# One step of Strassen's method in all six matrix products of a four-layer convolution kernel

## The chip, the cores and the metric

The kernel runs on one core of a Trainium2 chip. Its time is the device time of one execution in microseconds; the time before is the median of three runs. Profiles are of one execution each, and windows in them are counted from the start of the profiled span, which is some 2 us shorter than the device time.

## What is computed

The input is one image of 1024 channels by 64 x 64 pixels in f32. Four layers follow one another, each of the form `x = x + layer(group_norm(x))`:

```python
# layer 0: layer norm over the 64 x 64 of a channel, then a scan over the 1024 channels
dt  = softplus(einsum('bsdc,c->bsd', xn, dt_w) + dt_b)      # one decay per channel and image row
out = scan over s:  h = exp(-exp(log_A) * dt) * h + xn       # written as a masked product of cumsums
# layer 1 and layer 3: 1x1 convolution
out = einsum('oi,nihw->nohw', weight, x) + bias
# layer 2: input projection to 3 x 1024 channels, then a selective scan, then an output projection
x_ssm, res, gate = split(silu(in_proj_w @ x + b), 3)
xf  = silu(conv1d_3_taps(x_ssm))                             # along the 4096 pixels
dt, B, C = dbc_w @ xf + dbc_b                                # 2 heads x (1 + 8 + 8) rows
y   = selective_scan(xf, dt, B, C) in a data-dependent order of the pixels, per head
out = silu(out_proj_w @ (y * silu(gate) + res) + out_proj_b)
```

Six products of a 1024 x 1024 matrix with a 1024 x 4096 image carry nearly all of the arithmetic: layer 1, the three thirds of the input projection (x, res, gate), the output projection, layer 3.

## The kernel before

The image lies in SBUF throughout, as eight blocks `X[nb]` of 128 partitions x 8 channel tiles x 512 pixels (2 MB each). The program is written against a tile framework: its scheduler orders each engine's instructions by a cost estimate and by the order of the text, and it adds the waits; every engine then runs its own queue in order. Nearly all plain transfers are issued from the SP queue, indirect ones from GpSimd.

- **Layer 0** (lines 268 to 312): per block, ScalarE normalizes, TensorE transposes (`l0pt`) and sums the decay rows (`l0pd`), ScalarE and one small GpSimd add (`l0m`, L296) make the softplus, the result goes to HBM (`a_d`) and comes back broadcast (`l0a`, L302), VectorE scans (L304), TensorE transposes back (`l0pb`), VectorE adds into `X` and takes the statistics for the next norm (`take_stats`, L114).
- **Layers 1 and 3** (`pointwise`, L367): the whole weight matrix is loaded, then for each block and each of the eight output tiles `o` a group of eight matmuls over `k` fills one PSUM bank (`pm`), and one VectorE instruction (L387) adds bias and image back into `X`.
- **Ranking** (`rank_work`, L317): layer 2 needs the pixels in the order of a score. VectorE counts, for every pixel, the smaller scores (`hit`, L331; ties in `eq`, L342), in pieces of 1024 scores (`srow`). The steps are cut into a generator; `rank_steps` queues `each` of them behind a given instruction. In layer 1 there are 3 behind each of the 64 evictions, the rest lie in the x third of layer 2.
- **Layer 2, x third** (L435): eight tiles of output channels, each over the eight blocks, weights of one output tile at a time (`wt`). Per 128 x 512 result: silu, a conv of three taps on VectorE (L450, L453), silu, four transposes (`l2pt`, L462) and four matmuls with the block of pixels as the stationary side and the 34 columns of dt/B/C as the moving one (`l2pd`, L463), summed by VectorE over the eight tiles (L476). The transposed tokens go to HBM (`tok_d`).
- **Layer 2, res/gate and scan** (L517): 74 steps of the scan (`weigh`, `apply`) gather 128 tokens, build a 128 x 128 matrix on TensorE (`pr`, `pg`), VectorE, ScalarE and GpSimd (`cd`, L557), multiply (`py`) and scatter to `y_d`. Between them stand the res and gate products (`res_gate`), written to `res_d` and `sg_d`.
- **Layer 2, output** (L613): per block, `y`, `sg` and `rs` are loaded in eight tiles each, `y` is transposed (`ypt`), and eight groups of matmuls (`op`, L639) follow.

Every product of a 128 x 128 weight tile with 512 columns is one matmul call; f32 matmuls show as two records in the trace.

Of the kernel before, what the change touches and what calls it, by code (L numbers as in the profile page):

```python
# [23 lines left out]
NB = 8  # L24
# [14 lines left out]


_PAR = [("b1", CT), ("bin", OI), ("dww", 3 * CT), ("dwb", CT), ("bout", CT), ("b3", CT),
        ("logA", NB), ("lnw", NT), ("lnb", NT), ("dtw", 1), ("dtb", 1),
        ("Alog", S), ("D", 1), ("mob", 4 * HEADS), ("dbcb", HEADS * NF)]
# [19 lines left out]
def tile_net(ctx: ExitStack, tc: tile.TileContext, x, par_d, cst_d, w1_d, win_d, dbcw_d, wout_d, w3_d, out):  # L63
    nc = tc.nc
    const = ctx.enter_context(tc.tile_pool(name="const", bufs=1))
    xpool = ctx.enter_context(tc.tile_pool(name="xres", bufs=1))
    psum = ctx.enter_context(tc.tile_pool(name="psum", bufs=1, space=PSUM))
    phase = [None]
# [6 lines left out]
    def ps_mm(name):  # L75
        return ps_tile("mm", 3, name)

    def ps_tp(name):
        return ps_tile("tp", 2, name)

    def ps_g(name):
        return ps_tile("g", 2, name)

    def ps_y(name):
        return ps_tile("y", 1, name)

    x1_d = dram.tile([C, N], F32, name="x1_d")
# [19 lines left out]
    X = [xpool.tile([P, CT, FB], F32, name=f"X{nb}") for nb in range(NB)]  # L107
    for nb in range(NB):
        nc.sync.dma_start(X[nb], x[:, nb * FB : (nb + 1) * FB].rearrange("(ct p) n -> p ct n", p=P))  # L109
# [147 lines left out]
    for nb in range(NB):  # L257
        for ct in range(CT):
            take_stats(nb, ct)

# [6 lines left out]

    with tc.issue_after(exp_ln.ins), tc.tile_pool(name="l0", bufs=2) as l0, \
            tc.tile_pool(name="ps0", bufs=2, space=PSUM) as ps0:
        for nb in range(NB):  # L270
            xt = l0.tile([P, TPB, C], F32, tag="xt", name=f"l0xt{nb}")
# [39 lines left out]
            for ct in range(CT):  # L311
                take_stats(nb, ct)

# [53 lines left out]
    def pointwise(name, w_d, bias_name, each=0, store=None):  # L367
        scale, bias = group_norm(f"gn{name}")
        with tc.tile_pool(name=f"{name}w", bufs=1) as wp, tc.tile_pool(name=f"{name}x", bufs=12) as xp, \
                tc.tile_pool(name=f"{name}p", bufs=1, space=PSUM) as pp:  # L370
            phase[0] = pp
            w = wp.tile([P, CT, C], F32, name=f"{name}_w")
            for k in range(CT):
                nc.sync.dma_start(w[:, k, :], w_d[k])
            for nb in range(NB):
                xn = []
                for k in range(CT):
                    t = xp.tile([P, FB], F32, tag="xn", name=f"{name}xn{nb}_{k}")
                    nc.scalar.activation(t, X[nb][:, k, :], AF.Identity,  # L379
                                         bias=bias[:, k : k + 1], scale=scale[:, k : k + 1])  # L380
                    xn.append(t)
                for o in range(CT):
                    pm = ps_mm(f"{name}pm{nb}_{o}")
                    for k in range(CT):
                        nc.tensor.matmul(pm, w[:, k, o * P : (o + 1) * P], xn[k],  # L385
                                         start=(k == 0), stop=(k == CT - 1))
                    last = nc.vector.scalar_tensor_tensor(  # L387
                        X[nb][:, o, :], pm, pcol(bias_name, o), X[nb][:, o, :], ALU.add, ALU.add)
                    if store is None:
                        last = take_stats(nb, o)  # L390
                    rank_steps(each, last)
                dst = x1_d if store is None else store
                nc.sync.dma_start(dst[:, nb * FB : (nb + 1) * FB].rearrange("(ct p) n -> p ct n", p=P), X[nb])

    rank_pool = tc.tile_pool(name="rank", bufs=2, side="right")
    work = rank_work(rank_pool.__enter__())
# [6 lines left out]
    pointwise("l1", w1_d, "b1", each=3)  # L403


    ps2 = tc.tile_pool(name="ps2", bufs=1, space=PSUM)
    phase[0] = ps2.__enter__()
    scale2, bias2 = group_norm("gn2")
    for nb in range(NB):
        for ct in range(CT):  # L410
            sc, bi = scale2[:, ct : ct + 1], bias2[:, ct : ct + 1]
            if ct % 2 == 0:
                nc.scalar.activation(X[nb][:, ct, :], X[nb][:, ct, :], AF.Identity, bias=bi, scale=sc)
            else:
                nc.vector.tensor_scalar(X[nb][:, ct, :], X[nb][:, ct, :], sc, bi, ALU.mult, ALU.add)

    with tc.tile_pool(name="l2w", bufs=2) as l2w:

        def in_proj_weights(oc):
            wt = l2w.tile([P, CT, P], F32, tag="wt", name=f"wt{oc}")  # L420
            nc.sync.dma_start(wt, win_d[oc])
            return wt

        def in_proj(wt, oc, nb):
            pm = ps_mm(f"ip{oc}_{nb}")
            for k in range(CT):
                nc.tensor.matmul(pm, wt[:, k, :], X[nb][:, k, :], start=(k == 0), stop=(k == CT - 1))  # L427
            return pm


        with tc.tile_pool(name="l2a", bufs=2) as pa, tc.tile_pool(name="l2acc", bufs=1) as pacc:
            dbcw = pacc.tile([P, CT, HEADS * NF], F32, name="dbcw")
            nc.sync.dma_start(dbcw, dbcw_d)
            acc = pacc.tile([P, NT, HEADS * NF], F32, name="acc")
            for oc in range(CT):  # L435
                wt = in_proj_weights(oc)
                xs = pa.tile([P, N + 2], F32, tag="xs", name=f"xs{oc}", bufs=2)
                nc.vector.memset(xs[:, 0:1], 0.0)
                nc.vector.memset(xs[:, N + 1 : N + 2], 0.0)
                h, c0 = oc // 4, (oc % 4) * P  # L440
                for nb in range(NB + 1):
                    if nb < NB:
                        pm = in_proj(wt, oc, nb)
                        nc.scalar.activation(xs[:, 1 + nb * FB : 1 + (nb + 1) * FB], pm, AF.Silu,  # L444
                                             bias=pcol("bin", oc))
                    if nb == 0:
                        continue
                    j = nb - 1
                    cv = pa.tile([P, FB], F32, tag="cv", name=f"cv{oc}_{j}")
                    nc.vector.tensor_scalar(cv, xs[:, j * FB : (j + 1) * FB], pcol("dww", 3 * oc),  # L450
                                            pcol("dwb", oc), ALU.mult, ALU.add)
                    for t in (1, 2):
                        nc.vector.scalar_tensor_tensor(  # L453
                            cv, xs[:, j * FB + t : (j + 1) * FB + t], pcol("dww", 3 * oc + t), cv,
                            ALU.mult, ALU.add)
                    xf = pa.tile([P, FB], F32, tag="xf", name=f"xf{oc}_{j}")
                    nc.scalar.activation(xf, cv, AF.Silu)
                    pt = ps_tp(f"l2pt{oc}_{j}")
                    pd = ps_g(f"l2pd{oc}_{j}")
                    for q in range(TPB):  # L460
                        blk = xf[:, q * P : (q + 1) * P]
                        nc.tensor.transpose(pt[:, q * P : (q + 1) * P], blk, ident)  # L462
                        nc.tensor.matmul(pd[:, q * HEADS * NF : (q + 1) * HEADS * NF], blk, dbcw[:, oc, :],  # L463
                                         start=True, stop=True)
                    xt = pa.tile([P, TPB, P], F32, tag="xt", name=f"l2xt{oc}_{j}")
                    nc.scalar.copy(xt.rearrange("p q c -> p (q c)"), pt)
                    nc.sync.dma_start(
                        tok_d[h * N + j * FB : h * N + (j + 1) * FB, c0 : c0 + P].rearrange(
                            "(q p) c -> p q c", p=P), xt)
                    got = pd[:, : TPB * HEADS * NF].rearrange("p (q f) -> p q f", q=TPB)  # L470
                    at = acc[:, j * TPB : (j + 1) * TPB, :]
                    if oc == 0:
                        more = par[:, PAR["dbcb"]].unsqueeze(1).to_broadcast([P, TPB, HEADS * NF])
                    else:
                        more = at
                    last = nc.vector.tensor_tensor(at, got, more, ALU.add)  # L476

                    rank_steps(3, last)
            rank_steps(2 * NT * HEADS * CT, last)
            rank_pool.__exit__(None, None, None)  # L480


            with tc.tile_pool(name="l2f", bufs=1) as pf:
                for h in range(HEADS):
                    f = acc[:, :, h * NF : (h + 1) * NF]
# [31 lines left out]
        with tc.tile_pool(name="l2b", bufs=2) as pb, tc.tile_pool(name="l2h", bufs=1) as ph:  # L517
            G2 = [ph.tile([P, P], F32, name=f"G{i}") for i in range(2)]
            for g in G2:
                nc.gpsimd.memset(g, 0.0)  # L520
# [218 lines left out]
```

## Time and profile before

The median is 3389.95 us (3389.55 to 3391.72). The stages, from the trace:

| stage | from, us | to, us | TensorE busy, us | VectorE busy, us |
|---|---|---|---|---|
| load, statistics | 0 | 60 | 1.6 | 51.4 |
| layer 0 | 60 | 301 | 150.9 | 153.0 |
| layer 1 | 301 | 752 | 443.3 | 308.8 |
| layer 2, x third | 752 | 1300 | 533.6 | 300.0 |
| layer 2, res/gate and scan | 1300 | 2398 | 1091.7 | 303.4 |
| layer 2, output | 2398 | 2932 | 479.3 | 176.8 |
| layer 3 | 2932 | 3388 | 443.1 | 50.1 |

How to read the profile: a group of instructions names its line, engine and operation, what it writes and reads (`out<-in`), the shape, the number of records, the busy time, the mean time of one, and the idle time of its engine just before it with what ended that idle time. Matmuls overlap, so the time of one matmul is longer than the distance between two. The chain of waits is followed back from the last instruction; its rows are start, length, and what it was.

### The profile page before, as it was taken

The numbers are of one execution on the slowest core, as the hardware profiler recorded it, in microseconds if no ns is written. First come the engines' busy times: TensorE is split into PE (matmuls) and PEld (weight loads), VectorE is DVE, ScalarE is ACT, GpSimd is POOL, SyncE is SP. The second block draws the span as 40 slices with busy tenths as digits, with TensorE's granted clock in tenths as the row PEclk, the third lists the DMA queues.
The fourth block names the chain that finished last, engine by engine and source line by source line (L and its number), as shares of the span: only waits on it lengthen the run. The fifth ranks groups of instructions, "written<-read, shape, count | busy, mean of one in ns | idle before, by whom it ended". The sixth has DMA issues, their size and how long they took to land.

```text
span 3387.6 us, 23688 instructions
## 1 busy us (share of the span) xinstructions
PE 3143.4 (93%) x8417; PEld 1413.5 (42%) x8417; DVE 1343.5 (40%) x2744; ACT 924.4 (27%) x1242; POOL 328.3 (10%) x305
## 2 busy tenths in 40 slices
PE   2675999989999999999999999999699999999998
PEld 0333444444555554444444444444344444444443
DVE  6667777377775222222222222322133333211111
ACT  2661101004222223444444544554100000110100
POOL 0100000200002101222222222221000000000000
PEclk9886999999999999999999999999899999999999
DMA  5323011121111114222222222224723323101011
GB/s 206 89 71 98 32 55 53 34 64 38 44 44 47 38 41 77 82 73 77 76 78 79 77 73 73 86 73 152 271 75 110 114 75 116 65 25 50 36 39 50
DMA packets 190271, 258.91 MB, mean 76 GB/s; under 512 B 37817, under 2 KB 103673, under 8 KB 190154
## 3 DMA queue, kind: packets, MB, share of 16 engines
q1 hardware_dynamic: 176266, 216.70, 19.8%
q0 software_dynamic: 13888, 40.70, 3.7%
q8 instruction: 67, 1.10, 0.1%
q14 instruction: 50, 0.41, 0.0%
HBM read 152.10 MB, written 105.26 MB: 76 GB/s over the span
## 4 chain that ended last, share of the span: by engine, by line
PE 86%; DVE 5%; DMA 4%; ACT 2%; issue 1%; SPq 1%; POOL 0%; DVEq 0%; ACTq 0%; POOLq 0%
PE ip L427 38%; PE l3pm L385 13%; PE l1pm L385 13%; PE op L639 11%; PE pg L571 2%; PE py L584 2%; DMA sg<-sg_d 2%; DVE l0xt L304 1%; PE l0pd L286 1%; PE l2pd L463 1%; PE l0pb L308 1%; PE pr L550 1%; PE l2pt L462 1%; PE pr L551 1%; SPq L109 1%
## 5 line engine op out<-in xcount | busy, mean ns | idle before, releaser
L427 PE MATMUL ip<-X,wt 128*128 128x512 f32 x3072 | 1373.3, 599 | 9.5 <-ACT rg L531 5.2
L427 PEld LDWEIGHTS ip<-X,wt 128*128 128x128 f32 x3072 | 574.9, 191 | 738.0 <-issue 725.0
L639 PE MATMUL op<-ym,wo 128*128 128x512 f32 x1024 | 453.6, 596 | 13.9 <-DVE ym L634 13.7
L385 PE MATMUL l3pm<-l3xn,l_w 128*128 128x512 f32 x1024 | 442.5, 595 | 3.1 <-ACT l3xn L379 3.1
L385 PE MATMUL l1pm<-l1xn,l_w 128*128 128x512 f32 x1024 | 442.1, 595 | 3.2 <-ACT l1xn L379 3.2
L331 DVE TENSOR_SCALAR_CACHE_REDUCE hit<-srow,score 128x1024 bf16<-128x1024 f32 (+7 forms) x312 | 337.4, 1081 | 15.3 <-DMA srow<-score_d 10.2
L385 PEld LDWEIGHTS l3pm<-l3xn,l_w 128*128 128x128 f32 x1024 | 195.5, 191 | 249.3 <-issue 240.8
L385 PEld LDWEIGHTS l1pm<-l1xn,l_w 128*128 128x128 f32 x1024 | 195.4, 191 | 249.1 <-issue 241.4
L639 PEld LDWEIGHTS op<-ym,wo 128*128 128x128 f32 x1024 | 189.3, 191 | 238.0 <-issue 220.7
L387 DVE SCALAR_TENSOR_TENSOR X<-l3pm,par,X 128x512 f32<-128x512 f32 x64 | 48.0, 750 | 396.3 <-PE l3pm L385 359.6
L554 DVE COPY cts<-pr 16x64 f32<-16x64 f32 x74 | 16.0, 216 | 469.8 <-PE pr L551 469.8
L531 ACT ACTIVATE rg<-ip,par 128x512 f32<-128x512 f32 x128 | 87.8, 687 | 388.8 <-PE ip L427 270.2
L642 ACT ACTIVATE os<-op,par 128x512 f32<-128x512 f32 x64 | 44.0, 687 | 486.9 <-PE op L639 439.1
L114 DVE BATCH_NORM_STATS2 stats<-X 128x6 f32<-128x512 f32 x256 | 166.8, 686 | 6.4 <-DMA X<-in_x_dram 2.2
L453 DVE SCALAR_TENSOR_TENSOR cv<-xs,par,cv 128x512 f32<-128x512 f32 x128 | 95.9, 751 | 164.2 <-ACT xs L444 161.7
L379 ACT ACTIVATE l3xn<-X,gnl_bias,gnl_scale 128x512 f32<-128x512 f32 x64 | 50.8, 810 | 336.8 <-PE l3pm L385 332.7
L379 ACT ACTIVATE l1xn<-X,gnl_bias,gnl_scale 128x512 f32<-128x512 f32 x64 | 50.9, 812 | 336.5 <-PE l1pm L385 332.6
L531 ACT ACT_TABLE_LOAD x74 | 94.9, 1283 | 156.9 <-issue 156.2
L557 POOL TENSOR_TENSOR cd<-cts,cst 16x512 f32<-16x512 f32 x74 | 76.4, 1033 | 619.3 <-DVE cts L554 619.2
L643 DVE TENSOR_TENSOR X<-X,os 128x512 f32<-128x512 f32 x64 | 44.1, 689 | 220.6 <-ACT os L642 220.6
L547 DVE TENSOR_SCALAR ds<-cst,g 128x64 f32<-128x64 f32 x74 | 21.9, 295 | 268.0 <-DMA g<-tok_d,src 251.0
L444 ACT ACTIVATE xs<-ip,par 128x512 f32<-128x512 f32 x64 | 43.9, 690 | 241.8 <-PE ip L427 241.8
(192 smaller groups left out, 2408.6 us busy)
## 6 DMA issues: line engine op xcount, KB each, us to landing
X<-in_x_dram SPq DMA_DIRECT2D x8, 2048.0 KB
l0a<-a_d SPq DMA_DIRECT2D x64, 256.0 KB
x_d<-X SPq DMA_DIRECT2D x8, 2048.0 KB
tok_d<-l2xt SPq DMA_DIRECT2D x64, 256.0 KB
res_d<-rg SPq DMA_DIRECT2D x64, 256.0 KB
sg_d<-rg SPq DMA_DIRECT2D x64, 256.0 KB
X<-x_d SPq DMA_DIRECT2D x8, 2048.0 KB
yt<-y_d SPq DMA_DIRECT2D x64, 256.0 KB
```

The costliest lines, as they stand in the source:

```text
L114: return nc.vector.bn_stats(stats[:, ct, nb, :], X[nb][:, ct, :])
L331: nc.vector.tensor_scalar(hit[:, : hi - lo], srow[:, lo:hi], sn, None, op, ALU.add, accum_out=count[:, h, b, slot : slot + 1],)
L379: nc.scalar.activation(t, X[nb][:, k, :], AF.Identity, bias=bias[:, k : k + 1], scale=scale[:, k : k + 1])
L385: nc.tensor.matmul(pm, w[:, k, o * P : (o + 1) * P], xn[k], start=(k == 0), stop=(k == CT - 1))
L387: last = nc.vector.scalar_tensor_tensor(X[nb][:, o, :], pm, pcol(bias_name, o), X[nb][:, o, :], ALU.add, ALU.add)
L427: nc.tensor.matmul(pm, wt[:, k, :], X[nb][:, k, :], start=(k == 0), stop=(k == CT - 1))
L453: nc.vector.scalar_tensor_tensor(cv, xs[:, j * FB + t : (j + 1) * FB + t], pcol("dww", 3 * oc + t), cv, ALU.mult, ALU.add)
L531: nc.scalar.activation(r, pm, AF.Silu, bias=pcol("bin", oc))
L557: nc.gpsimd.tensor_tensor(cd, cts.unsqueeze(1).to_broadcast([HEADS * S, S, LC]), eye8.unsqueeze(2).to_broadcast([HEADS * S, S, LC]), ALU.mult)
L571: nc.tensor.matmul(pg, bts, cd.rearrange("p s t -> p (s t)"), start=True, stop=True)
L584: nc.tensor.matmul(py, G, g[:, :DH], start=True, stop=True)
L639: nc.tensor.matmul(pm, wo[:, k, o * P : (o + 1) * P], ym[k], start=(k == 0), stop=(k == CT - 1))
```

## The change

All six products are done by one step of Strassen's method in Winograd's form over pairs of blocks. The weight matrix is cut into 2 x 2 quarters A11 to A22, the 1024 x 1024 pair of image blocks into B11 to B22 (rows: halves of the channels, columns: the two blocks). Seven products of halves stand for eight. It is for a smaller number of matmuls. The sums of weight quarters are made on the chip, once per matrix, by GpSimd (`sum_weights`), and go to HBM (`s_d`); the sums of image quarters (`t1` to `t4`) are made per pair (`b_sets`), by GpSimd, for a stage's first pair mostly by VectorE. The sums of products are made partly in PSUM, where a later product is accumulated on an earlier one, and partly at eviction: every output tile is written once (`put`) and added to once (`add`).

With it come: weights streamed in pieces of 512 KB, one per product, in six buffers (`weights`); only four of the eight image blocks in SBUF, the others kept in HBM (`x0_d`, `x1_d`, `x2_d`) and loaded again, with the pairs taken in alternating order so that those at hand come first (`EARLY`, `LATE`); four PSUM banks for the products, two sets of two; `each=4` rank steps behind an add in layer 1, the rest behind the convs of the x third; dt/B/C with the 34 columns as the stationary side and the pixels as the moving one, accumulated in PSUM over the eight tiles and transposed afterwards.

```diff
-    xpool = ctx.enter_context(tc.tile_pool(name="xres", bufs=1))
+    xpool = ctx.enter_context(tc.tile_pool(name="xres", bufs=4))
+    wpool = ctx.enter_context(tc.tile_pool(name="wts", bufs=6))
...
+    def sum_weights(m, pool):
+        for g in range(NG):
+            def t(name, src=None):
+                w = pool.tile([P, KH * OG * P], F32, tag=f"s_{name}", name=f"s{m}_{g}_{name}", bufs=1)
+                if src is not None:
+                    nc.gpsimd.dma_start(w, src)
+                return w
+
+            a = [t(f"a{i}", w_d[m, g, i]) for i in range(4)]
+            s3 = t("s3")
+            nc.gpsimd.tensor_tensor(s3, a[0], a[2], ALU.subtract)
+            nc.gpsimd.tensor_tensor(a[2], a[2], a[3], ALU.add)
+            nc.gpsimd.tensor_tensor(a[0], a[2], a[0], ALU.subtract)
+            nc.gpsimd.tensor_tensor(a[1], a[1], a[0], ALU.subtract)
+            for d, w in zip(s_d[m][g], (a[2], a[0], s3, a[1])):
+                nc.gpsimd.dma_start(d, w)
...
+    sum_weights(W1, sum_pool[1])
     with tc.issue_after(exp_ln.ins), tc.tile_pool(name="l0", bufs=2) as l0, \
             tc.tile_pool(name="ps0", bufs=2, space=PSUM) as ps0:
         for nb in range(NB):
+            if nb >= NB // 2:
+                load(nb, x)
...
+            if nb < NB // 2:
+                save(nb, x0_d)
...
+        def comb(name, out, one, two):
+            eng = nc.vector if first and name != "t3" else nc.gpsimd
+            B[name] = B[out] if out else [b_tile(name, k, B["name"]) for k in range(KH)]
+            for k in range(KH):
+                eng.tensor_tensor(B[name][k], B[one][k], B[two][k], ALU.subtract)
...
+            def product(to, i, name, fresh):
+                w = weights(m, g, i)
+                for o in range(OG):
+                    for k in range(KH):
+                        nc.tensor.matmul(to[o], w[:, k, o * P : (o + 1) * P], B[name][k],
+                                         start=(fresh and k == 0), stop=(k == KH - 1),
+                                         skip_group_check=True)
...
+            b = banks(two, 2)
+            product(b, 1, "b21", True)
+            out(put, 0, 0, b)
+            yield
+            a = banks(one, 1)
+            product(a, 0, "b11", True)
+            out(add, 0, 0, a)
+            yield
+            b = banks(two, 3)
+            product(b, 6, "b22", True)
+            out(put, 0, 1, b)
+            yield
+            product(a, 4, "t2", False)
+            out(put, 1, 0, a)
+            yield
+            b = banks(two, 7)
+            product(b, 5, "t3", True)
+            out(put, 1, 1, b)
+            yield
+            product(a, 3, "t1", False)
+            out(add, 0, 1, a)
+            out(add, 1, 1, a)
+            yield
+            product(b, 2, "t4", False)
+            out(add, 1, 0, b)
...
+    pointwise("l1", W1, "b1", LATE + EARLY, x0_d, x1_d, each=4)
...
+            nc.tensor.matmul(dbc[nb][: HEADS * NF, :], dbcw[:, o, :], xf,
+                             start=(count == 0), stop=(count == CT - 1))
...
+        units = run(LATE + EARLY, [WR, WG], normed(norm2), put2b, add2b, before2)
...
+        for _ in run(EARLY + LATE, [WO], make_y, put2c, add2c, before2, after2c):
```

In layers 1 and 3 both `put` and `add` are VectorE instructions. In layer 2 `put` is a ScalarE copy out of PSUM, `add` a VectorE addition; silu follows the addition.

## The prediction

> **What bounds the kernel now.** I read the page's busy line first, then its chain by engine, then the groups (shapes kept apart), then the windows, one per stage, and last the timelines of layer 0.
>
> ```profile
> PE 3143.4 (93%) x8417; PEld 1413.5 (42%) x8417; DVE 1343.5 (40%) x2744; ACT 924.4 (27%) x1242; POOL 328.3 (10%) x305
> PE 86%; DVE 5%; DMA 4%; ACT 2%; issue 1%; SPq 1%; POOL 0%; DVEq 0%; ACTq 0%; POOLq 0%
> ```
> TensorE is busy for 93% and 86% of the chain. A busy matmul row proves little by itself, so the next view matters more: the pitch.
>
> ```profile
> L427 PE MATMUL ip<-X,wt 128*128 128x512 f32 x3072 | 1373.3, 599 | 9.5 <-ACT rg L531 5.2 <-ACT X L413 3.0 <-ACT xs L444 1.3
> L385 PE MATMUL l1pm<-l1xn,l_w 128*128 128x512 f32 x1024 | 442.1, 595 | 3.2 <-ACT l1xn L379 3.2
> L331 DVE TENSOR_SCALAR_CACHE_REDUCE hit<-srow,score 128x1024 bf16<-128x1024 f32 x200 | 254.3, 1272 | 14.2 <-DMA srow<-score_d 10.2
> L463 PE MATMUL l2pd<-dbcw,xf 128*128 128x34 f32 x512 | 75.4, 239 | 0.0
> L296 POOL TENSOR_TENSOR l0m<-l0m,l0e 8x1024 f32<-8x1024 f32 x8 | 18.8, 2344 | 240.5 <-ACT l0e L295 240.5
> ```
> ```profile
> 853.80 6.95 PE ip L427 x16
> 861.87 6.95 PE ip L427 x16
> ```
> An f32 matmul leaves two records; 16 records (8 matmuls) take 6.95 us, 0.434 us each, with almost no idle before them. The mean of 599 ns is latency, not pitch. In the chain (last two lines: start, length) 1.12 us lie between two such blocks, the transposes and dt/B/C matmuls of one conv block.
>
> ```profile
> 0.00:60.00 60.00, 1.61 (x5) 1.13 (x5) 51.44 (x161) 3.39 (x8) 1.10 (x7) 1.00 0.80 291
> 301.00:752.00 451.00, 443.27 (x1028) 196.41 (x1028) 308.76 (x625) 51.11 (x65) 31.12 (x32) 0.99 0.13 45
> 752.00:1300.00 548.00, 533.63 (x1822) 275.58 (x1823) 300.03 (x628) 150.46 (x235) 33.41 (x33) 0.98 0.17 48
> 1300.00:2398.00 1098.00, 1091.67 (x2616) 451.56 (x2614) 303.43 (x823) 488.60 (x635) 243.87 (x225) 1.00 0.28 89
> 2398.00:2932.00 534.00, 479.31 (x1282) 218.25 (x1282) 176.82 (x267) 45.59 (x66) 0.00 (x0) 0.97 0.33 109
> 2932.00:3388.00 456.00, 443.07 (x1026) 196.04 (x1026) 50.06 (x76) 51.05 (x65) 0.00 (x0) 0.98 0.12 44
> ```
> Columns: PE, PEld, DVE, ACT, POOL busy, clock, DMA share, GB/s. Rows: load, layer 1, the x third of layer 2, its res/gate thirds with the scan, its output product, layer 3. Layer 0 (60 to 301) is the one stretch without a full engine. Note layer 1: VectorE already works 309 of 451 us, mostly rank counting (hit).
>
> ```profile
> 85.35 2.33 POOL L296 TENSOR_TENSOR l0m<-l0m,l0e 8x1024 f32<-8x1024 f32 x1 [80.58 <-ACT l0e L295]
> 244.75 2.35 POOL L296 TENSOR_TENSOR l0m<-l0m,l0e 8x1024 f32<-8x1024 f32 x1 [33.95 <-ACT l0e L295]
> ```
> Each image block of layer 0 passes through one small GpSimd add. GpSimd comes to it early and waits; it is never late.
>
> **What the Trainium skill says.** GPSIMD Engine Reference, section 3.1: a two-input tensor_tensor costs about 2.6 cycles an element, 4497 ns for 2048. The trace agrees: 2344 ns for 1024 a partition. DMA: Bandwidth & Descriptors, Anatomy of one DMA: a GpSimd-issued DMA costs about 2.0 us fixed plus its bytes at 436 GB/s, so 3.2 us for 512 KB (estimate); the trace has no direct DMA from GpSimd, but its indirect ones land in 2.7 and 3.8 us (median). Same page, Queues, rings and completion order: an engine takes a queue's descriptors in ring order, so a small load issued behind a 2 MB one on the SP queue waits for it; no run shows it yet.
>
> **Part by part.** *Matmuls.* 7 products for 8: 6144 records become 5376; 768 x 0.434 = 333 us off TensorE: 55.5 in each of layer 1, x, output and layer 3, 111 in res/gate.
>
> *dt/B/C as stationary side.* Per conv block four 34-column matmuls become one 512-column one (2 x 0.434 = 0.87) beside the four transposes (about 0.43 of the 1.12): 1.30 for 1.12, 64 times: +12 us. The VectorE sums it removes were hidden.
>
> *Weights streamed.* 336 loads of 512 KB, one per 6.95 us product, 75 GB/s, six buffers, so asked for some 35 us ahead. The load stage moves 291 GB/s. Hidden: 0. Half-resident image: some 60 MB more transfers; within the products hidden by prefetch; only layer 0 pays (below).
>
> *Sets of column sums.* 16 subtractions of 128x512 per pair, GpSimd, 1.17 us each (half of 2.34), within the last four products: 19 of 28 us. The first pair's 12 on VectorE at 0.69 (as L634 and L643) lie beside the first three products. 0.
>
> *Weight sums, layer 0.* The built order of GpSimd's instructions puts the 12 groups of sums among the eight l0m adds: 4 3/4 groups stand ahead of the first, about one more ahead of each next, all 12 ahead of the sixth. Behind a delayed l0m wait exp, a_d, the a loads, the scan on VectorE and layer 1. A group: four loads (issue 1 us each, as the indirect ones, landing 3.2), four adds 4 x 2.34, four stores, each buffer reused only after its store: about 22 us alone, 28 while the image loads. So the first l0m comes at 5 + 28 + 28 + 22 + 22 + 18 = 123 instead of 85, the sixth at 277 instead of 208. Then the l0 buffers' own rhythm (two blocks in 54 us), plus the SP order: the save of a block and the reload that waits for it stand ahead of the next a loads, about 14 us twice. Together I put layer 0's end at 367 instead of 301: +66. Bounds: 18 us a group with no SP effect +40; 35 us a group, sixth l0m at 408, +165.
>
> *Layer 1.* Each quadrant is now evicted twice: 64 put (0.75, as L387) + 64 add (0.69, as L310) + 64 stats (0.61 apart, eight in 4.84 in the timeline): 131 us instead of 87. And four rank steps follow each add, so of the 391 us of counting (L331 337.4 and L342 22.3, with their accumulator reads 25.9 and 5.3) the built order leaves about 310 in layer 1. With the 12 first subtractions VectorE has some 450 us of work against 387 us of products (896 x 0.434), in one queue: an eviction behind 4 counts (1.32 each) holds a PSUM bank, of which there is one spare product. VectorE becomes the bound: 450 + 20 where TensorE is behind + 15 for the srow loads that it meets unhidden = 485 instead of 451. At the end about 20 more counts lie among the group norm's steps: 25 us before x can start. +34 +20 = +54.
>
> *x third.* 389 + 64 x 1.30 = 472 of TensorE, plus some 35 of stalls: after each last product four conv blocks come at once, 4 x 2.04 us of VectorE, with few matmuls between: 507. With the norm's lead-out taken above: 548 -> 511, and the 15 us gap at 1300 closes because res products no longer wait for the scan's data: -52.
>
> *res/gate.* 1098 - 111 = 987, plus 35 (estimate): the cd path (VectorE copy, GpSimd product) has 1.8 us of slack per step and VectorE and GpSimd now carry more: -76.
>
> *Output product.* 534 - 55, and the loads of y, sg and res come 16 tiles at once: 16 x 0.77 MB at 300 GB/s, 41 us, beside four products of 28: three times 10 us, once 25; against that the eight waits of before (some 45) go: 488, -46.
>
> *Layer 3.* 456 - 55 + 1: 402, -54.
>
> Sum: 3390 + 66 + 54 - 52 - 76 - 46 - 54 = 3282. The stall terms (35 + 35 + 55 + 20 + 15 = 160) are the ones most easily under-rated, since they come from single queues looked at alone; I add a fifth of them, 33 us, for queues that meet: 3315.
>
> **Rivals.** A: TensorE stays the bound everywhere, VectorE and GpSimd keep out of its way: 3390 - 333 + 12 = 3069, to 3150 with layer 0's lower bound. For it: the idle of every engine but TensorE. Against: 450 us of VectorE in layer 1. B, slower: groups of sums cost 35 us (+165 in layer 0, 99 over mine) and the cd and conv stalls double (+70): 3484; a milder form, one of the two, 3400 to 3440. For it: GpSimd's queue is in order and unproven with direct DMAs. Against: DMA is 1 to 30% busy in layer 0. C: the weight stream falls behind on SP, behind stores that wait, half a microsecond per product: 336 x 0.5 = +168, 3483. Against: six buffers. D: gains and losses cancel to within 7 us.
>
> **How the numbers follow.** Forecast (VectorE-bound layer 1, late layer 0, 3200 to 3380) 0.62; A 0.12; D 0.04; B 0.15, C 0.07. Faster 0.74, same 0.04, slower 0.22. The range leaves out A's lower part and the worst of B and C: 3200 to 3430.
>
> **What would show it.** Right: l0m's idle turns from ACT l0e to GpSimd work, first l0m near 123; in layer 1 VectorE near 95% busy over 480 us and TensorE waiting for VectorE; matmul records 5376 at 0.43; res/gate near 1005. Wrong: layer 1 near 390 us (A), SP-fed weights as the releaser of matmuls (C), groups far from 22 us.

## The result, and the profile after

The changed kernel takes 3413.6 us (median of 4 runs, 3409.9 to 3413.8), the kernel before 3390.6 us: a ratio of 1.0065, 95% interval 1.0048 to 1.0083. It is slower by 0.65%. 3315 us and "faster" were predicted.

The page of the changed kernel, its busy line and TensorE's row of the slices:

```profile
PE 2898.8 (85%) x7315; PEld 1249.7 (37%) x7315; DVE 1672.5 (49%) x3195; ACT 1074.1 (31%) x1558; POOL 849.3 (25%) x708
PE   0454598896579699999989999998998999989999
```

TensorE is busy for 245 us less, where 321 less were expected (333 of matmuls, with 12 more for dt/B/C), and its share fell from 93% to 85%. The slices say where the idle time sits: in the first 40% of the span. To be cut alike in every kernel, the stages are taken here from fixed events: the first matmul of each group norm's statistics (image, layer 0, layer 1), ScalarE's first eviction of a res product, the first matmul of layer 3's group norm, the end. Windows at these cuts, two of the kernel before and then those of the changed kernel (us; busy PE, PEld, DVE, ACT, POOL; granted TensorE clock; DMA share; GB/s):

```profile
303.70:755.30 451.60, 443.27 (x1028) 196.41 (x1028) 309.39 (x623) 51.11 (x65) 31.12 (x32) 0.99 0.13 45
755.30:1314.40 559.10, 543.56 (x1844) 279.66 (x1844) 298.39 (x628) 152.94 (x238) 35.17 (x36) 0.99 0.17 47
```
```profile
0.00:82.70 82.70, 0.45 (x2) 0.15 (x2) 57.00 (x147) 3.17 (x6) 42.64 (x44) 1.00 1.00 381
82.70:412.70 330.00, 163.39 (x645) 83.01 (x645) 170.81 (x195) 133.91 (x172) 155.17 (x116) 0.71 0.68 224
412.70:921.60 508.90, 410.71 (x901) 175.18 (x901) 425.15 (x873) 50.65 (x65) 97.37 (x84) 0.92 0.33 113
921.60:1536.50 614.90, 525.65 (x1366) 219.30 (x1366) 293.36 (x547) 235.70 (x373) 115.69 (x90) 0.92 0.34 102
...
3014.20:3411.90 397.70, 388.54 (x900) 171.95 (x900) 104.31 (x153) 50.60 (x65) 65.50 (x52) 0.99 0.39 130
```

The lengths at the same cuts, beside the terms of the prediction:

| stage | before | after | measured | predicted |
|---|---|---|---|---|
| image, layer 0 | 55.8 + 247.9 | 82.7 + 330.0 | +109 | +66 |
| layer 1 | 451.6 | 508.9 | +57 | +54 |
| x third | 559.1 | 614.9 | +56 | -52 |
| res, gate, output | 1617.0 | 1477.7 | -139 | -122 |
| layer 3 | 456.2 | 397.7 | -58 | -54 |
| queues that meet | | | | +33 |

The second half pays what was promised, and a little more. The pitch, the distance from one matmul record to the next, is the predicted one; the chain of waits ends with this piece of layer 3:

```profile
3040.34 367.65 PE mm L476 x856
```

That is 0.430 us a record, without a gap. This pitch does not hold behind a wait. TensorE near the start of the x third, in order of time:

```profile
968.53 1.12 PE L644 MATMUL l2pt<-cst,xf 128*128 128x128 f32 x4 [10.76 <-ACT xf L641]
969.57 1.92 PE L649 MATMUL dbc<-xf,dbcw 128*34 128x512 f32 x2
971.42 1.74 PE L476 MATMUL mm<-t,w 128*128 128x512 f32 x2
972.99 0.60 PE L644 MATMUL l2pt<-cst,xf 128*128 128x128 f32 x4
973.52 1.05 PE L649 MATMUL dbc<-xf,dbcw 128*34 128x512 f32 x2
974.50 20.87 PE L476 MATMUL mm<-t,w 128*128 128x512 f32 x48
```

After a wait of 10.76 us the same four transposes and two dt/B/C matmuls take 1.12 and 1.92 us, and 4.5 us later 0.60 and 1.05. So a wait costs more here than its own length. Over a stage it shows in the windows: layer 1 and layer 3 have the same 900 records, but TensorE is busy for 411 us in one, at a granted clock of 0.92, and for 389 in the other, at 0.99.

The first half loses 222 us where 68 were expected (101 with the term for meeting queues). The waits of the whole run show the candidates (engine, line, released by: us in total, times, longest):

```profile
DVE l0xt L353 <- DMA l0a<-a_d: 117.6, 7, 53.4
ACT l2xt L652 <- DMA tok_d<-l2xt: 45.4, 6, 36.1
PE pg L820 <- POOL cd L806: 42.7, 15, 13.1
PE mm L476 <- DVE X L561: 41.7, 12, 23.3
DVE hit L382 <- DMA srow<-score_d: 41.0, 6, 25.4
```

In none of them does a matmul wait for its weights: layer 0's scan waits for its rows, a copy of the x third for its store, the scan's matmul of the res/gate stretch for GpSimd, layer 1's products for VectorE's evictions, the ranking for its score rows.

### The profile page after: what moved, and what is told of

Read it like the earlier page. It is cut to its first block, busy times and chain, and to the rows that moved or that the text cites. A ratio compares the mean times of both kernels' runs of the same rounds, so it can differ in the third digit from the quotient of the medians.

```text
span 3411.9 us, 23831 instructions
## 1 busy us (share of the span) xinstructions
PE 2898.8 (85%) x7315; PEld 1249.7 (37%) x7315; DVE 1672.5 (49%) x3195; ACT 1074.1 (31%) x1558; POOL 849.3 (25%) x708
## 5 line engine op out<-in xcount | busy, mean ns | idle before, releaser
L476 PE MATMUL mm<-t,w 128*128 128x512 f32 x3072 | 1366.7, 597 | 48.9 <-DVE X L561 39.6
L476 PE MATMUL mm<-b,w 128*128 128x512 f32 x2304 | 1053.4, 610 | 47.6 <-DVE X L565 23.0
L476 PEld LDWEIGHTS mm<-t,w 128*128 128x128 f32 x3072 | 575.9, 191 | 794.6 <-issue 725.0
L476 PEld LDWEIGHTS mm<-b,w 128*128 128x128 f32 x2304 | 441.8, 195 | 631.8 <-issue 570.2
L438 POOL TENSOR_TENSOR t<-t,b 128x512 f32<-128x512 f32 x140 | 192.5, 1392 | 1332.7 <-ACT t L547 629.6
L561 DVE SCALAR_TENSOR_TENSOR X<-mm,par,X 128x512 f32<-128x512 f32 x128 | 95.0, 748 | 196.9 <-PE mm L476 185.9
L438 POOL TENSOR_TENSOR t<-b,t 128x512 f32<-128x512 f32 x120 | 158.9, 1340 | 2.2
L353 DVE TENSOR_TENSOR_SCAN l0xt<-l0a,l0xt 128x1024 f32<-128x1024 f32 x32 | 86.3, 2701 | 117.6 <-DMA l0a<-a_d 117.6
L781 ACT ACTIVATE rg<-rg,par 128x512 f32<-128x512 f32 x128 | 89.3, 718 | 147.5 <-DVE rg L780 147.3
L790 POOL DMA_INDIRECT g<-tok_d,src x74 | 88.0, 1189 | 129.7 <-PE py L833 117.5
```

The costliest lines, as they stand in the source:

```text
L353: nc.vector.tensor_tensor_scan(xt[:, q, :], a, xt[:, q, :], 0.0, ALU.mult, ALU.add)
L438: eng.tensor_tensor(B[name][k], B[one][k], B[two][k], ALU.subtract)
L476: nc.tensor.matmul(to[o], w[:, k, o * P : (o + 1) * P], B[name][k], start=(fresh and k == 0), stop=(k == KH - 1), skip_group_check=True)
L561: nc.vector.scalar_tensor_tensor(part, ps, pcol(bias_name, o), part, ALU.add, ALU.add)
L781: nc.scalar.activation(r, r, AF.Silu, bias=pcol("bin", (m - WX) * CT + o))
L790: nc.gpsimd.indirect_dma_start(out=g[:, :], out_offset=None, in_=tok_d[:, :], in_offset=bass.IndirectOffsetOnAxis(ap=src[:, k : k + 1], ax ...
```

## The experiments

Stage lengths in us at the cuts above, of the profiled execution; the time is the median of the timed runs.

| kernel | image | layer 0 | layer 1 | x third | res to output | layer 3 | time |
|---|---|---|---|---|---|---|---|
| changed | 82.7 | 330.0 | 508.9 | 614.9 | 1477.7 | 397.7 | 3413.6 |
| e9_anchor_only | 81.7 | 334.8 | 508.4 | 576.4 | 1476.9 | 397.8 | 3379.0 |
| e1_rank_3_3 | 82.2 | 327.2 | 437.0 | 619.9 | 1479.4 | 397.5 | 3341.3 |
| e5_anchor | 81.7 | 341.1 | 436.7 | 592.7 | 1479.8 | 397.8 | 3326.7 |
| e3_idx_pool | 80.7 | 327.1 | 493.0 | 591.4 | 1479.6 | 397.6 | 3375.5 |
| e6_sub_vector | 80.9 | 333.1 | 509.7 | 590.7 | 1438.1 | 397.8 | 3349.5 |
| e2_m_vector | 82.4 | 312.5 | 509.7 | 610.9 | 1475.4 | 397.8 | 3393.1 |
| e4_sums_late | 75.3 | 273.5 | 541.9 | 614.7 | 1476.2 | 397.8 | 3381.8 |
| e7_no_sums | 55.7 | 273.5 | 510.7 | 610.1 | 1477.1 | 397.5 | 3326.4 |
| e8_no_sums_gp | 55.5 | 277.5 | 510.6 | 618.7 | 1477.5 | 397.7 | 3339.9 |
| c1_combined | 81.7 | 310.8 | 436.3 | 561.1 | 1441.7 | 397.5 | 3235.1 |
| c2_combined_late | 75.2 | 279.6 | 490.4 | 560.7 | 1440.5 | 397.6 | 3244.7 |
| c4_combined_gp | 75.3 | 279.6 | 488.6 | 559.9 | 1442.9 | 397.5 | 3243.8 |

Stages that an edit does not touch repeat: layer 3 within 0.4 us, res to output within 5, layer 1 within 3 (508 to 511), the x third between 610 and 619 (the changed kernel, e2, e4, e7, e8). Layer 0 is looser: 327 to 341 us in six kernels (the changed one, e1, e3, e5, e6, e9) that have the same work there, so differences under some 14 us in layer 0 are not read, and the 18 us of e2 only as a size.

**Ranking, how much of it in layer 1.** The change had raised it from 3 to 4 units (steps of the ranking) per addition.

```diff
-    pointwise("l1", W1, "b1", LATE + EARLY, x0_d, x1_d, each=4)
+    pointwise("l1", W1, "b1", LATE + EARLY, x0_d, x1_d, each=3)
...
-            rank_steps(2, last)
+            rank_steps(3, last)
```

> Undoes one part: the ranking is spread as before the change (3 units behind each closing addition of layer 1 and 3 behind each convolution of the x third, not 4 and 2). The change has 256 of the 322 units in layer 1, this one 192. Theory V (VectorE sets layer 1's length): 64 units of about 1.6 us leave it, layer 1 (417 to 935 us in the changed kernel, 518 us) takes about 420 and the x third (608 us, VectorE busy some 40% of it) does not grow: about 3320 us. Theory M (the work only moves, because the x third is held by VectorE's queue as well): layer 1 shrinks by 60 to 100 us, the x third grows by as much: 3395 to 3420. Theory P (layer 1 waits for its own chain of bank, addition and next product, not for the ranking): layer 1 stays above 490 us, total above 3390.

Measured: 3341.3 us, ratio to the kernel before 0.985 (0.983 to 0.986). Layer 1 lost 72 us (theory V had expected 98), the x third kept its length. VectorE's busy time in layer 1 fell from 425 of 509 us to 352 of 437, so theory V holds: VectorE set layer 1's length. TensorE is now busy for 393 of the 437. Two things went along with the spread. The wait for score rows in layer 1 fell from 38 us to 7, and the run below that takes this wait away alone gains 16 us there, so some 56 of the 72 (an estimate, if the two add) are VectorE's work. In the x third the 64 added units met a shorter wait for the token stores (1.5 us at most, not 36.1), so its equal length is a balance and does not show that the units are free there.

**Ranking, what it is queued behind in the x third.** `rank_steps(n, behind)` only orders instructions of the engine that `behind` ran on. Before the change that was a VectorE addition; in the changed kernel it is a ScalarE copy, so the counts, which run on VectorE, are tied to nothing and go wherever VectorE's queue takes them early.

```diff
             for t in (1, 2):
-                nc.vector.scalar_tensor_tensor(cv, xo[:, at + t ...
+                last = nc.vector.scalar_tensor_tensor(cv, xo[:, at + t ...
...
-            last = nc.scalar.copy(xt.rearrange("p q c -> p (q c)"), pt)
+            nc.scalar.copy(xt.rearrange("p q c -> p (q c)"), pt)
```

> The changed kernel with one thing put back: in the x third the ranking units are queued behind the convolution's last VectorE operation, not behind ScalarE's copy. Still 4 and 2 units. Theory H: x third 615 to 590 to 600 us, total 3390 to 3402; less than in the 3-and-3 spread (27 us), since only 66 units and what layer 1 left over are there to be spread. Theory C: within 6 us of 3413.6.

> The 3-and-3 spread again (3341.3 us by itself), and in the x third the units are queued behind the last VectorE operation of each convolution, as before the change, not behind ScalarE's copy l2xt, which holds nothing on VectorE. Theory H (in the x third the counts run ahead in VectorE's queue, up to 26 in a row, and hold the additions that free TensorE's banks): the x third, 620 us in the 3-and-3 run, falls to 560 to 580, layer 1 stays at 437, total 3280 to 3305. Theory C (the x third is held by the chain of convolution, sigmoid and transposes with its few buffers, wherever the counts stand): x third 605 or more, total above 3325.

Alone (4 and 2 units), this edit takes 38.5 us off the x third and 34.6 off the whole: 3379.0 us, ratio 0.9968 (0.9957 to 0.9978), more than theory H had expected. Moving one anchor is enough to turn the change from a loss of 0.65% into a gain of 0.3%. Not all of it is blocks of counts: TensorE's longest wait in the x third, which comes from the SyncE queue (next experiment), was 35.4 us in the changed kernel and is 11.4 here. With the 3-and-3 spread the anchor gave 27 us in the x third, less than the 40 to 60 that H asked for, and 14.7 in the whole, so that neither theory's numbers were met; the profiled execution had a layer 0 of 341 us, 14 more than e1's. The timeline of VectorE in the changed kernel, near the start of the x third:

```profile
972.89 1.28 DVE L382 TENSOR_SCALAR_CACHE_REDUCE hit<-srow,score 128x1024 bf16<-128x1024 f32 x1
974.21 1.28 DVE L382 TENSOR_SCALAR_CACHE_REDUCE hit<-srow,score 128x1024 bf16<-128x1024 f32 x1
...
998.11 0.35 DVE L382 TENSOR_SCALAR_CACHE_REDUCE hit<-srow,score 128x128 bf16<-128x128 f32 x1
998.50 0.35 DVE L399 TENSOR_REDUCE rank<-count 128x32 f32<-128x192 f32 x1
998.88 0.18 DVE L401 CAST rank_i<-rank 128x32 int32<-128x32 f32 x1
998.98 1.28 DVE L672 TENSOR_TENSOR xs<-mm,xs 128x512 f32<-128x512 f32 x2
```

For 26 us VectorE does nothing but count and close the ranks of a head; only then come two additions that free banks. The first 65 us of x products in the changed kernel, then in the kernel with the anchor alone (columns as in the windows above):

```profile
935.00:1000.00 65.00, 49.31 (x110) 20.86 (x110) 61.61 (x118) 20.42 (x32) 7.23 (x5) 0.89 0.37 128
```
```profile
938.00:1003.00 65.00, 61.87 (x146) 25.34 (x145) 38.98 (x62) 25.81 (x41) 6.46 (x4) 0.94 0.43 145
```

VectorE has 62 us of work in one and 39 in the other, TensorE 110 records and 146.

**Loads of the permutation.** The scatter of the ranks runs on GpSimd, 32 indirect stores for each half of the heads; the loads that read it back stood on SyncE.

```diff
-                nc.sync.dma_start(idx[r0 : r0 + LT, : NK - 1],
+                nc.gpsimd.dma_start(idx[r0 : r0 + LT, : NK - 1],
...
-                nc.sync.dma_start(idx[r0 : r0 + N - full, NK - 1 :], perm_d[h][full:])
+                nc.gpsimd.dma_start(idx[r0 : r0 + N - full, NK - 1 :], perm_d[h][full:])
```

> The four loads of the permutation into src and dst (for each half of the heads) are issued from GpSimd, behind the scatter that they wait for, not from SyncE. Theory S (on SyncE they stand ahead of score rows, weights and token stores and hold them until the scatter ends): VectorE's longest wait for a score row falls from 25 to under 10 us, the 36 us wait of ScalarE's l2xt in the x third goes, and the total falls by 40 to 60 us, to 3355 to 3375. Theory N (those waits come from the stores of 127 partitions or from the scatter itself): the 36 us stay and the total is within 8 us of 3413.6.

Measured: 3375.5 us, 38 less, just short of what theory S asked for; the x third 24 less, layer 1 16 less. The longest wait for a score row fell from 25.4 to 3.5 us and that of the copy l2xt from 36.1 to 2.6. In the changed kernel the SyncE queue shows the reason:

```profile
1128.81 0.35 SPq L412 DMA_DIRECT2D src<-perm_d  x1
1129.21 3.02 SPq L414 DMA_DIRECT2D src<-perm_d  x1
1132.28 0.32 SPq L412 DMA_DIRECT2D dst<-perm_d  x1
1132.64 1.94 SPq L414 DMA_DIRECT2D dst<-perm_d  x1
1134.68 0.22 SPq L654 DMA_DIRECT2D tok_d<-l2xt  x1
```

The load of src waits for the last scatter on GpSimd (issued at 1126.39), and behind it stands the store of a copy that ScalarE had made at about 1087. With its two buffers full, ScalarE stops, and TensorE waits 35.4 us for the silu (`xf`) that ScalarE can't start. In layer 1 the loads of the other head's permutation hold a score row in the same way, VectorE's 25.4 us, and behind it TensorE waits the 23.3 us listed above; in this kernel the longest such wait is 2.8. Theory S holds; the 127-partition stores of theory N are still there in this kernel and cost nothing like it.

**Subtractions of layer 2 on VectorE.**

```diff
-            eng = nc.vector if first and name != "t3" else nc.gpsimd
+            eng = nc.vector if first == 2 or (first and name != "t3") else nc.gpsimd
...
-                ... first=(i == 0))
+                ... first=(i == 0) or 2 * (mats[0] in (WX, WR)))
```

> The changed kernel, but the 12 subtractions per pair of blocks in layer 2's x, res and gate products all run on VectorE, none in bursts on GpSimd. Theory G (while GpSimd subtracts, VectorE's own operations take several times as long, so each burst of some 20 us costs TensorE about 11 us): the x third falls by 25 to 35 us (615 before) and the res/gate stretch by 25 to 40 (1056 before), total 3345 to 3365. Theory B (what costs is that the next pair's blocks come late, on whichever engine): both within 8 us, total 3400 to 3420.

The edit moves 48 subtractions in each of the two stages, 16 for every pair after the first, not 12; of the first pair `t3` stays on GpSimd.

Measured: 3349.5 us, ratio to the kernel before 0.9875 (0.9855 to 0.9894): 24 us in the x third, 40 in the res/gate stretch. The sizes are about those of theory G, but its mechanism sets the time in the x third alone. There the convolution's operations, from a view of their tile in the changed kernel and then in this one (min, median, max in ns):

```profile
L632 DVE SCALAR_TENSOR_TENSOR cv<-xs,par,cv x128: 733/747/9194, 965.9 to 1517.0; 128x512 f32<-128x512 f32 x128
```
```profile
L632 DVE SCALAR_TENSOR_TENSOR cv<-xs,par,cv x128: 740/749/758, 964.6 to 1495.1; 128x512 f32<-128x512 f32 x128
```

An operation of 0.75 us takes up to 9.2 us while GpSimd subtracts. The longest one stands in the first burst, where TensorE waits for the SyncE queue in any case (40.7 us in this run too). The gain is in the other two: in the changed kernel TensorE waits 7.7 and 7.0 us for ScalarE's silu in them, behind stretched convolutions, and runs at the slower pace after it; in this run none of them is over 0.3 us. The Trainium skill, GPSIMD Engine Reference, Specifications, gives GpSimd's SBUF interfaces as shared with VectorE, with contention for VectorE instructions that have two SBUF inputs or run in a 2-port mode; the convolution step has two (xs and cv), and this case agrees. Operations that read one SBUF tile were stretched as well (a copy of 0.17 us to 1.24, the convolution's first step of 0.55 to 1.58); no run shows in which mode they ran.

In the res/gate stretch VectorE's operations are stretched too, but by some 5 us over the whole stage. TensorE waits there for GpSimd's queue. The timelines of GpSimd and of TensorE in the changed kernel:

```profile
1764.36 1.27 POOL L438 TENSOR_TENSOR t<-t,b 128x512 f32<-128x512 f32 x1
...
1782.11 3.69 POOL L438 TENSOR_TENSOR t<-b,t 128x512 f32<-128x512 f32 x3
1785.77 1.03 POOL L806 TENSOR_TENSOR cd<-cts,cst 16x512 f32<-16x512 f32 x1
```
```profile
1786.85 2.07 PE L820 MATMUL pg<-cd,bts 16*128 16x512 f32 x2 [10.33 <-POOL cd L806]
```

The product cd of one scan step stands behind the 16 subtractions, and TensorE waits 10.33 us for it (the modelled end of the matmuls before hides some more). It happens three times, 10.3 to 13.1 us each, 35 us together. With the subtractions elsewhere the longest wait for cd is 1.7 us.

**Weight sums in layer 0.** Four kernels: l0m off GpSimd, the sums later, no sums (plain blocks of weights in their place), and no sums with the saves and reloads off SyncE and l0m on VectorE.

```diff
-                nc.gpsimd.tensor_tensor(m, m, e, ALU.add)
+                nc.vector.tensor_tensor(m, m, e, ALU.add)
```

> One line: the addition l0m of layer 0 goes from GpSimd to VectorE; the weight sums, their loads and stores stay where they are. Theory Q (layer 0 is held by the place of l0m behind a group of sums in GpSimd's queue): layer 0 ends at 330 to 350 us, not 417, and the total is 3330 to 3350. Theory D (it is held by the 41 MB that the sums move in layer 0, which delay the image, the rows l0a and the reloads): layer 0 still ends after 395 us and the total is above 3390.

```diff
-    for m in (WX, WR, WG, WO, W3):
-        sum_weights(m, sum_pool[1])
+    sums = (s for m in (WX, WR, WG, WO, W3) for s in sum_weights(m, sum_pool[1]))
...
+            adds[0] += 1
+            if not last and adds[0] % 6 == 0:
+                with tc.issue_after(pool_last[0].ins):
+                    next(sums, None)
```

> The sums of the five matrices after layer 1's are issued in layer 1, a group behind every sixth closing addition, not in layer 0. Theory Q and D agree that layer 0 shrinks; if only the queue counts, its end is that of the run with l0m on VectorE, within 10 us; if the transfers count too, it is earlier by 20 us or more (about 310 us against 340). Cost to look for: subtractions of the next pair of blocks that wait on GpSimd behind a group (22 to 28 us each, up to 3 pairs). Total about 3310 to 3330 if those are hidden, 3380 if not.

```diff
-        d = w_d[m, g, (0, 1, 3)[i]] if i < 3 else s_d[m][g][i - 3]
+        d = w_d[m, g, (0, 1, 3, 0, 1, 2, 3)[i]]
...
-    sum_weights(W1, sum_pool[1])
```

> Leaves out all 12 groups of weight sums; the four products that use a sum take a plain weight block of the same size in its place, so that the multiplications and the weight stream keep their number. Price of the sums as a whole. Theory Q+D (queue and transfers in layer 0 are the sums' doing): the image is normed at 56 us as before the change (83 in the changed kernel), layer 0 takes 245 to 260 us, not 330, total 3300 to 3320. Theory R (a good part of layer 0's growth is the half-resident image, its saves and reloads ahead of the rows l0a): layer 0 still takes 280 us or more, total above 3340.

```diff
-                load(nb, x)
+                load(nb, x, nc.gpsimd)
...
-                save(nb, x0_d)
+                save(nb, x0_d, q=nc.gpsimd)
```

> Again without the 12 groups of weight sums (plain blocks in their place), where layer 0 took 273.5 us against 247.9 before the change; now the image saves and reloads of layer 0 are issued from GpSimd, and l0m runs on VectorE so that it is not behind them. Theory O (the order on SyncE: a save and the reload that waits for it stand ahead of the next rows l0a): layer 0 takes 245 to 255 us, total 3300 to 3312. Theory T (the transfers themselves, 8 saves and reloads of 2 MB beside the image's weights, and the reload's late landing): 268 us or more, total above 3320.

Without the sums the image is normed at 55.7 us, as before the change, and layer 0 takes 273.5: the sums cost 27 + 56 us. The 273.5 and the 3326.4 lie between theory Q+D and theory R, so each has a part. Of the 56, GpSimd's queue is the smaller piece: with l0m on VectorE layer 0 still takes 312.5, so 18 us, and that total, 3393.1, is theory D's. The other 39 come with the groups themselves, their transfers or their additions beside VectorE's scans; no run parts the two. The scans can be summed: the 32 of them took 86 us in the changed kernel, 77 without sums and 73 in the last kernel, where GpSimd adds nothing in layer 0, so their stretching is some 9 us of the 39. Moving ten groups to layer 1 gives the whole 56 back in layer 0, and costs 33 us of layer 1; its total is the one expected if that cost is not hidden. What is left of layer 0's growth, 26 us, stays without sums. It is not the order on SyncE (theory O): issued from GpSimd, the same saves and reloads leave 277.5. What it is instead (theory T names the transfers and the late landing of the reload) is not shown.

**Together.** The combined kernel has the 3-and-3 spread with its anchor, the permutation loads on GpSimd, and l0m and the subtractions of x, res and gate on VectorE.

> All mends that kept the result together: ranking 3 and 3 with its anchor on VectorE, permutation loads on GpSimd, l0m on VectorE, subtractions of layer 2 on VectorE; the weight sums stay in layer 0. If the savings add (72 + 45 + 38 + 20 + 50 us): 3190. If the x third's share is counted twice, since three of the mends work there: 3220 to 3260. More VectorE work in the x third could make it the bound: above 3280.

> The combined kernel (3235.1 us) with the sums of five matrices moved from layer 0 into layer 1, a group behind every sixth closing addition. With the 4-unit ranking that move gave layer 0 57 us and image 7, and took 33 in layer 1, where VectorE was the bound. With 3 units VectorE has some 85 us of slack there. If slack hides the collisions: 3180 to 3190. If they cost as much as before: 3205 to 3215.

> The same with layer 0's image saves and reloads issued from GpSimd, behind the two groups of sums for layer 1 that are still made while the image loads. Theory O: 18 to 25 us under the run without this, theory T: within 8 us of it, or above it where the saves wait behind the sums.

The combined kernel takes 3235.1 us, ratio to the kernel before 0.9535 (0.9519 to 0.9551): 4.7% faster than before and 178 us under the changed kernel. The savings do not add, since three of them mend the same x third; the time is the one expected for that case. The late sums took 54 us in layer 1 for the 38 that they gave before it, so neither number expected for them held: VectorE is idle for 125 of those 490 us, but the subtractions of the next pair wait on GpSimd behind a group (TensorE 12.9 us at once for one of them). Not all of the 54 is taken apart. Saves and reloads from GpSimd changed nothing here either.

## Why the prediction was wrong

*Matmuls* (-333): right in number and in pitch, where TensorE runs on. Layer 3, which has nothing else to do, gave 58 us where 54 were expected. The prediction took the pitch as the same everywhere; behind waits it is not, which made TensorE's work 22 us longer in layer 1 alone.

*dt/B/C* (+12): mis-sized. Four transposes and two dt/B/C matmuls take 1.51 us (972.99 to 974.50), not 1.30, so some 25 us against the 1.12 of before.

*Layer 1* (+54): right in size, with the named bound, and partly by luck in its parts. From its first product to its last it took 482 us, and 485 had been put; but VectorE worked 401 of them, not 450, and waited 40 for TensorE and 38 for score rows, not 20 and 15. One of the score rows was held by the permutation loads on SyncE.

*x third* (507 us, -52): the step that failed. From its first product on it took 601 us. TensorE was idle for 77 of them, where 35 of stalls had been put, and busy for 510, where 472 had been put, without the 14 us of res products at the end of the stage (an estimate: 32 records at 0.43). Of the 38 us more of work, 13 are the mis-sized dt/B/C; the rest fits the slower pace behind the waits, at a granted clock of 0.92 where it was 0.99. Three causes of the waits were shown, which overlap: counts that run ahead of the additions (38 us alone, in part through a shorter wait on SyncE), the loads of the permutation on SyncE (24), the bursts on GpSimd (24). All three mended and 64 more ranking units in it, the stage takes 561, and the clock is 0.98. The prediction put down four conv blocks at once as the only cause of stalls. It knew that "about 20 more counts lie among the group norm's steps" and stopped there; it read the built order of VectorE for layer 1 and not for the x third, where the trace shows blocks of counts ahead of the additions. That the anchor had moved to another engine stands in the kernel's text.

*Sets of column sums* (0): wrong. "Within the last four products: 19 of 28 us" asked whether the burst ends in time for the next pair, not what shares GpSimd or its memory access meanwhile. It cost 24 us in the x third and 40 in res/gate; layer 3 and the output product took no longer than predicted, and layer 1's bursts were not moved.

*res/gate, output* (-122): measured -139; cut at the first eviction of an output product it is -75 and -64, where -76 and -46 were predicted. The 35 us put on the cd path were the right place and near the 40 that moving the bursts gave; the path suffers from the burst in GpSimd's queue, though, not from 1.8 us of lost slack per step. The 55 us of load collisions in the output product were too many.

*Weight sums, layer 0* (+66): mis-sized, +109. The first l0m came at 122.2 us (123 predicted), the sixth at 325.1 (277): a group took 26.5 us on average, 19 to 33 (eleven from 15.88 to 307.18), not 22. But GpSimd's queue, on which most of the sum rested, was worth only some 18 us. The image loads 27 us later beside the sums, which the prediction had not followed through to the norm; 39 us more in layer 0 come with the groups in other ways, and 26 stay without them, beside the half-resident image, about the "14 us twice", though not through the order on SyncE.

*Queues that meet* (+33): the guess was right in kind and about a quarter of what was needed. By the table the misses are 108 in the x third, 43 up to the end of layer 0 and 3 in layer 1; less 22 of a better second half and the 33, they are the 99 us between 3315 and 3413.6.

Rival A fell with layer 1. Rival B gave the time in its milder form (3400 to 3440) and half of the cause: the stalls of the x third doubled, from 35 to 77 us, but those around cd did not, and a group cost 26.5 us, not 35. Rival C did not occur: no matmul waits for a weight load among the waits listed. Rival D, within 7 us of the kernel before, misses by 16.

## What to carry to other kernels

Work that fills idle time needs its anchor on the engine that it runs on, and its place in the built queue must be looked at in every stage, not only where most of it lies. Before a burst of cheap work goes to a quiet engine, list what else that engine does in the same stretch and who waits for it: here some 20 us of subtractions, in time for their own user, cost TensorE 10 to 13 us each time in the res/gate stretch. Count a wait of TensorE as more than its length, as the work behind it ran slower here. A load that waits for another engine belongs in the queue behind what it waits for; in a queue shared with stores and streams it stops them all.

## What the runs showed of the hardware

Behind a wait of 10.76 us TensorE's four transposes took 1.12 us and two dt/B/C matmuls 1.92, and 0.60 and 1.05 us when it had run for 4.5 us; layer 1's granted clock was 0.92 with its waits and 0.97 in the run with the 3-and-3 spread. A convolution step of 0.75 us on VectorE stretched to 9.2 us beside GpSimd's subtractions, and a scan of 2.29 us to 4.59 beside GpSimd's sums; without the sums two scans still took 4.02 and 4.08, beside the small l0m of 2.3 us on 8 partitions, and with no arithmetic on GpSimd none took over 2.3. GpSimd's own subtraction of 128x512 had a median of 1.27 us and a maximum of 3.97. The additions xs, which read one input from PSUM, kept 0.67 to 0.69 us throughout. A direct load issued by GpSimd held it 0.53 us and landed in 6.9 us (512 KB, layer 0 busy), not the 3.2 that had been estimated.
